# One kernel, one edit: where weight differences are taken and which queue carries a table

## The chip, the core and the metric

The kernel runs on one core of a Trainium2 chip. Its time is the device time of one execution in microseconds (us). A core has a matrix engine (TensorE, PE in the profile, with its weight loads as PEld), VectorE (DVE), ScalarE (ACT), GpSimd (POOL) and SyncE (SP). The engines run side by side, each takes its own instructions strictly in order, and they wait for each other through semaphores. SP computes nothing here; it issues transfers (DMAs). ACT can issue transfers too, from the same instruction stream that holds its activations and copies.

## What is computed

Only the first block of the reference matters for this change: three approximate matrix products ("amm"), each with a softmax over 16 codewords, with batch normalisation between them. The edit touches the first two of the three.

```python
def _amm(patches, centroids, lut, inv_temp):
    v = patches.reshape(B, ncb, sub, H * W).transpose(0, 3, 1, 2)
    scores = 2.0 * einsum('blcs,cks->blck', v, centroids) - sum(centroids * centroids, -1)
    attn = softmax(scores * inv_temp, axis=-1)
    out = einsum('blck,cko->blo', attn, lut)
...
out = _amm(x, c1_centroids, c1_lut, c1_invt)                    # layer 1
out = relu(_bn(out, bn1_g, bn1_b))
out = _amm(_extract3x3(out, 1), c2_centroids, c2_lut, c2_invt)  # layer 2
out = relu(_bn(out, bn2_g, bn2_b))
out = _amm(out, c3_centroids, c3_lut, c3_invt)
```

Since the 16 weights of a softmax add up to one, the kernel replaces the first 15 rows of every table block by their difference to row 15. Row 15 then drops out of the product, and its place is used for rows of another block.

## The kernel before

**Units.** Layer 1 and layer 2 are each cut into 128 units: 16 pairs of images times 8 tables. For unit u, PE makes scores (L910 in layer 1, L1056 in layer 2, four PSUM banks of the pool `sc`), ACT takes exponentials into a tile t (L576, four activations), DVE transposes and sums (L588, L607), takes reciprocals and spreads them (L609, L619), POOL multiplies (L621, L626), and PE multiplies the tile by table u % 8 (L748, 16 passes for four blocks or 12 for three). Six tiles t are in use; scores run four units ahead of the products.

**Rows.** Row 15 of each block of t is filled from a spare tile by SP: `spare_rows`, L725 (one transfer) or L728 (three transfers, for units 0, 4, 8, ...). A product can't begin before the rows of its own unit have landed.

**Tables.** `packed_lut` gives five steps for table b. `own` loads the 512 KB table (L692 in layer 2, four transfers of 128 KB). `less` takes the differences: two PE products of 128x512 with `less_last` (L700), each copied back over the table by ACT (L701). `keep` (only for b = 0 and 4) writes one block of the differenced table to DRAM (L704), and `others` reads rows of it into row 15 of the blocks of the other tables (L707). The products of table b need `less` of b and `others` of b. The PSUM of `less` comes from the pool `po` (3 banks) for b < 4, and from the 4 banks of `sc` for b > 3, the same banks that the scores use.

**Order in layer 1.** Steps are hung on the loop index i of `units` with `at(i, ...)`; the list at L858 gives the index at which table b is differenced. Within one i the order is: scores of unit i + 4, softmax and rows of earlier units, the steps hung on i, then a product. The products follow the rule `{-2: 0, -1: -1, 0: 1, 1: 2, 2: -1}`: unit 0 at i = -2, none at -1, unit 1 at 0, unit 2 at 1, none at 2, unit 3 at 3.

**Order in layer 2.** The input is first written to DRAM with borders (`store_pair`: an ACT activation at L990 into `pad`, then three SP transfers at L1002) and then read back as shifted patches (`load_patches`, L1012: six transfers per unit, four patch buffers). The first two units' patches are issued from SP and ACT together (`both`), all others from SP. `store_pair(0, 1)`, which units 4 to 7 need, is in `second_half` at i = -3; `more_tables` at i = -2 holds `others` of tables 2 and 3 and `own` of table 7. `side2` takes the differences of tables 4 to 7 at i = -3, -2, -1 and 0. `score2(u)` first issues the patches of unit u + 3 for u > 1, ahead of the rows that the same i issues.

**Completion semaphores.** The program gives transfers of SP and ACT eight completion semaphores in turn. So a transfer waits, besides its data, for the transfer that had its semaphore before, which in this stretch is the one eight issues earlier, on whichever of the two queues that was.

`exact` is a second pass of the same code that runs only if an overflow is found; it is not taken in the executions shown.

Of the kernel before, what the change touches and what calls it, by code (L numbers as in the profile page):

```python
# [149 lines left out]
def conv_preact_kernel(ctx: ExitStack, tc: tile.TileContext, a: dict, out: bass.AP):  # L150
    nc = tc.nc
    x = a["x"]
    B = x.shape[0]
    NP = B // 2
# [266 lines left out]
    lut2_tiles = a["lut2"].rearrange("(b c j e k) w -> b c (e k) j w", b=8, c=4, j=4, k=KC)  # L421
# [85 lines left out]
    def layers(exact, early=None):  # L507
# [151 lines left out]
        kept = two.enter_context(tc.tile_pool(name="p12x", bufs=1, side="right"))  # L659
# [19 lines left out]
        def packed_lut(layer, b):  # L679


            v = weights[b].rearrange("p (s w) -> p s w", s=4)
            kept = tables[2 * layer - 2 + b // 4].rearrange("(c k) w -> c k w", k=KC)
            j0 = 0 if b % 4 else 1
            k0 = b % 4 - 1 if b % 4 else 3

            def own():
                if layer == 1:
                    nc.sync.dma_start(v, lut1_tiles[b].rearrange("j c k w -> (c k) j w"))
                    return  # L690
                for c in range(4):
                    nc.sync.dma_start(v[32 * c : 32 * c + 32], lut2_tiles[b, c])  # L692

            def less():
                for h in range(2):
                    t = weights[b][:, 512 * h : 512 * h + 512]
                    ps = scores(512) if b > 3 else None
                    if ps is None:
                        ps = ps_po.tile([P, 512], F32, tag="po", name="less")
                    nc.tensor.matmul(ps, less_last, t, start=True, stop=True)  # L700
                    nc.scalar.copy(t, ps)  # L701

            def keep():
                nc.sync.dma_start(tables[2 * layer - 2 + b // 4], v[:, 0])  # L704

            def others():
                nc.sync.dma_start(v[15::16, j0:], kept[:, k0 : k0 + 13 - 4 * j0 : 4])  # L707

            return v, own, less, keep, others


# [82 lines left out]
        with ExitStack() as s:  # L794
# [56 lines left out]
            luts2 = [packed_lut(2, b) for b in range(8)]  # L851
# [3 lines left out]
                    at(8 * p + c - AHEAD - 1 - (p == 0), normalise(p, c))  # L855
            at(24, edges)
            at(40, masks2)
            for b, i in enumerate((-4, -4, -3, -3, -1, 0, 0, 1)):  # L858
                for k in (2, 3, 4):
                    if k != 3 or b % 4 == 0:  # L860
                        at(i, lambda b=b, k=k: luts[b][k]())
# [110 lines left out]
        with ExitStack() as s:  # L972
            st = s.enter_context(tc.tile_pool(name="p2tt", bufs=1 if exact else 2))
            once = s.enter_context(tc.tile_pool(name="p2c", bufs=1))
            luts3 = []

            NPB = 4
            SPAN = 2 * IMG - LEAD
            pbuf = []
            for k in range(NPB):  # L980
                t = once.tile([P, 4, 2 * IMG], F32, tag=f"patch{k}", name=f"patch{k}")
                nc.gpsimd.memset(t, 0.0)
                pbuf.append(t)
                if k == 0:
                    bn_final(once, stats1, 1, [1], sc1, bi1)
                    add_up(0, 8 * NP)

            def store_pair(p, h, engines=(nc.sync,)):
                t = pads[h]
                nc.scalar.activation(  # L990
                    t.rearrange("p (i r c) -> p i r c", r=15, c=15)[:, :, :14, :14],
                    out1[:, h, p * N2 : (p + 1) * N2].rearrange(
                        "p (i r c) -> p i r c", r=14, c=14
                    ),
                    AF.Relu,
                    bias=bi1[:, h : h + 1],
                    scale=sc1[:, h : h + 1],
                )
                for x in range(3):
                    c0 = LEAD + 2 * p * IMG + 1 - x  # L1000
                    v = h1d[x // 2][h, :, :, c0 : c0 + 2 * IMG]
                    engines[x % len(engines)].dma_start(v[:, x::2] if x < 2 else v, t)  # L1002

            def load_patches(u, engines=(nc.sync,)):
                p, b = divmod(u, 8)
                h, g = divmod(b, 4)
                for n, (src, rows) in enumerate(zip(h1d, (8, 16))):
                    for dy in range(3):  # L1010
                        c0 = LEAD + 2 * p * IMG + 15 * (dy - 1)
                        engines[dy % len(engines)].dma_start(  # L1012
                            pbuf[u % NPB][tap_row(dy, 2 * n) :: rows, :, :SPAN],
                            src[h, 4 * g : 4 * g + 4, :, c0 : c0 + SPAN].rearrange(
                                "q r n -> r q n"
                            ),
                        )

            both = nc.sync, nc.scalar
            store_pair(0, 0)  # L1020
            luts2[0][2]()
            luts2[1][2]()
            load_patches(0, engines=both)
            load_patches(1, engines=both)
            luts2[0][3]()
            luts2[2][2]()
            luts2[3][2]()
            load_patches(2)
            luts2[0][4]()
            load_patches(3)  # L1030

            def second_half():
                store_pair(0, 1)
                luts2[1][4]()
                if not exact:
                    load_patches(NPB)

            def more_tables():
                luts2[2][4]()
                luts2[3][4]()  # L1040
                luts2[7][1]()

            if exact:
                second_half()
                more_tables()
            w9, bias2 = parts[2]

            def score2(u):
                if u > (0 if exact else 1) and u + NPB - 1 < 8 * NP:
                    load_patches(u + NPB - 1)  # L1050
                scs = [scores(N2) for j in range(4)]
                for c in range(4):
                    for j, sc in enumerate(scs):
                        r = slice(32 * j, 32 * j + 27)
                        v = pbuf[u % NPB][r, c].rearrange("p (i r c) -> p i r c", r=15, c=15)
                        nc.tensor.matmul(  # L1056
                            sc[32 * c : 32 * c + 32],
                            w9[r, u % 8 * 4 + c],
                            v[:, :, :14, :14],
                            start=True,  # L1060
                            stop=True,
                        )
                return scs

            ahead = 1 if exact else 4

            def side2(i):

                if i == 1 - ahead and not exact:
                    second_half()  # L1070
                if i == 2 - ahead and not exact:
                    more_tables()
                for b in range(4, 8):
                    if i == max(b - 7, -ahead):
                        luts2[b][2]()
                    if i == max(b - 4, 0):
                        luts2[b][4]()
                if i == max(-2, -ahead):
                    luts2[4][3]()
                p = {4: 1}.get(i + ahead, (i + ahead + 9) / 8)  # L1080
                if p in range(1, NP):
                    for h in range(2):
                        store_pair(int(p), h)
                if i == 60:
                    bias3, biases = score_biases(ps_tr, big, st, 3, raw[3], P, 2, mask8, 4)
                    parts[3] = score_matrices(big, 3, "", raw[3], mask8), bias3
                    parts["biases3"] = biases
                if i == 64:
                    parts["biases3"]()
                next_lut3(i - 8 * (NP - 1) - 1)  # L1090

            def next_lut3(b):
                if b >= 0:
                    luts3.append(load_lut(b, a["lut3"][b * P : (b + 1) * P]))


            out2 = out1
            stats2 = big.tile([P, 2, NP, 6], F32, tag="stats", name="stats2")
            units(
                ahead,  # L1100
                ts,
                st,
                [v for v, *_ in luts2],
                score2,
                bias2,
                out2,
                stats2,
                side2,
                lambda h: bn_final(once, stats2, 2, [h], sc2, bi2),
                halve=not exact,  # L1110
            )
            next_lut3(7)
            add_up(1, 8 * NP)
# [402 lines left out]
    with ExitStack() as s:  # L1516
# [20 lines left out]
        for k in range(2):  # L1537
            t = once.tile([P, CT, LY], F32, tag=f"y{k}", name=f"y{k}")
            v = t[:, :, LEAD : LEAD + 2 * IMG]
# [562 lines left out]
        def store(p, h, xt, rank):  # L2102
# [33 lines left out]
            k0=41,  # L2136
# [167 lines left out]
```

## Time and profile before

| | us |
|---|---|
| median of 3 runs | 3368.95 |
| lowest and highest run | 3367.61, 3372.37 |
| the profiled execution, its own time | 3369.36 |
| its span, first to last instruction | 3367.6 |
| PE busy in it | 3297.9 (98%) |
| PE waits for a table of L692 (L700) | 6.7, one wait |
| PE waits for rows (L748 for t<-spare) | 5.5, four waits |
| mean granted TensorE clock | 0.994 |

A busy engine in this profile is one that has an instruction in flight. PE is busy nearly all the time, so in the two layers concerned the end can only move by what PE idles, or by the stretches in which its granted clock is halved. Both are found at the start of layer 1 (20 to 66 us from the start of the span) and at the start of layer 2 (826 to 910 us).

### The profile page before, as it was taken

Reading aid. Unit: us, or ns where it says so; the run is one execution under the profiler, and the core shown is the slowest. Engines: PE = TensorE matmul, PEld = TensorE weight load, DVE = VectorE, ACT = ScalarE, POOL = GpSimd, SP = SyncE. Lnnn points to the kernel's source line nnn. Section 1 sums busy time; section 2 is a strip of 40 time slices with the busy share of each in tenths; the row PEclk is TensorE's granted clock in tenths of the full one; section 3 lists DMA queues with packets and bytes.
Section 4 is the critical chain, followed back from the end, with each engine's and each line's share of the span. In section 5 each row is a group of like instructions: output and inputs, shape, how many; then the busy total and the mean of one; then the engine's idle time right before and its main releaser. Section 6 shows DMA issues by size and latency. Waiting matters only on the chain. (4 is left out here: it accounts for less than half of the span.)

```text
span 3367.6 us, 61031 instructions
## 1 busy us (share of the span) xinstructions
PE 3297.9 (98%) x22287; PEld 2011.5 (60%) x22287; DVE 2868.9 (85%) x4174; ACT 1788.6 (53%) x4419; POOL 2528.4 (75%) x1562
## 2 busy tenths in 40 slices
PE   7999999999899999999999999998999999999999
PEld 4555555554345444444478888885666666666665
DVE  8999999997788898888666667655899999999996
ACT  4555555554444444444311111107888888888886
POOL 5999999997688888888532222215988888888888
PEclk9999999999999999999999999999999999999999
DMA  4110111102444344343231111113233333232321
GB/s 120 47 49 28 46 47 34 40 28 78 136 126 122 112 120 123 109 125 109 69 81 50 50 50 39 50 47 125 67 88 98 90 89 98 78 91 84 93 81 49
DMA packets 242253, 266.34 MB, mean 79 GB/s; under 512 B 32812, under 2 KB 239700, under 8 KB 241944
## 3 DMA queue, kind: packets, MB, share of 16 engines
q1 hardware_dynamic: 241128, 261.85, 26.4%
q8 instruction: 180, 2.95, 0.4%
q14 instruction: 129, 1.06, 0.1%
q10 hardware_dynamic: 816, 0.48, 0.1%
HBM read 171.01 MB, written 75.58 MB: 73 GB/s over the span
## 5 line engine op out<-in xcount | busy, mean ns | idle before, releaser
L626 POOL TENSOR_TENSOR t<-t,r 128x1568 f32<-128x1568 f32 (+5 forms) x292 | 962.1, 3296 | 527.7 <-issue 222.7
L748 PE MATMUL po<-t,lut 128*128 128x392 f32 x3840 | 1332.2, 500 | 6.9 <-DMA t<-spare 5.5
L748 PEld LDWEIGHTS po<-t,lut 128*128 128x128 f32 x3840 | 710.6, 190 | 605.5 <-issue 81.3
L1811 PE MATMUL mm<-y,lut 128*128 128x392 f32 x2048 | 714.6, 494 | 2.0 <-DVE k L1827 2.0
L588 DVE STREAM_TRANSPOSE tt<-t 128x1568 f32<-128x1568 f32 (+1 forms) x284 | 517.4, 1822 | 158.5 <-ACT t L576 155.2
L576 ACT ACTIVATE t<-sc,cbias 128x392 f32<-128x392 f32 (+1 forms) x624 | 322.4, 597 | 557.0 <-PE sc L910 190.8
L2035 DVE SCALAR_TENSOR_TENSOR pa<-y,lepe_w,pa 128x406 f32<-128x406 f32 x900 | 536.4, 637 | 19.3 <-PE pa L2017 17.0
L619 DVE STREAM_TRANSPOSE r<-rc 128x1568 f32<-128x1568 f32 (+1 forms) x284 | 520.8, 1834 | 11.6 <-POOL t L626 1.2
L1811 PEld LDWEIGHTS mm<-y,lut 128*128 128x128 f32 x2048 | 369.4, 188 | 243.7 <-issue 6.3
L591 POOL TENSOR_TENSOR tt<-tt 128x784 f32<-128x784 f32 x252 | 463.5, 1839 | 24.0 <-DVE tt L588 21.5
L576 ACT ACTIVATE t<-sc,room 128x392 f32<-128x392 f32 x512 | 259.0, 588 | 391.9 <-issue 164.7
L1393 PE MATMUL po<-t,lut 128*128 128x224 f32 (+2 forms) x1352 | 313.3, 414 | 0.0
L607 DVE TENSOR_REDUCE sm<-tt 128x98 f32<-128x784 f32 (+2 forms) x284 | 297.0, 1046 | 1.3 <-POOL tt L591 0.8
L1393 PEld LDWEIGHTS po<-t,lut 128*128 128x128 f32 (+1 forms) x1352 | 233.4, 189 | 62.9 <-issue 60.6
L609 DVE RECIPROCAL rc<-sm 128x98 f32<-128x98 f32 (+1 forms) x284 | 220.1, 775 | 9.8
L630 ACT ACTIVATE sm<-sm 128x98 f32<-128x98 f32 (+1 forms) x284 | 85.1, 300 | 159.0 <-DVE rc L609 159.0
L1997 POOL TENSOR_TENSOR qr<-qr,zb 128x784 f32<-128x784 f32 x64 | 118.2, 1856 | 49.0 <-DMA zb<-zd 48.7
L1664 ACT ACTIVATE w<-x,tb,gn_a 128x196 f32<-128x196 f32 x248 | 128.4, 518 | 35.4 <-POOL y L1546 28.3
L1823 ACT ACTIVATE e<-e 128x392 f32<-128x392 f32 x256 | 134.4, 525 | 1.0
L1777 ACT ACTIVATE y<-x,gb,ga 128x196 f32<-128x196 f32 x256 | 123.3, 541 | 12.6 <-POOL gb L1740 12.6
L1406 DVE TENSOR_TENSOR o<-po,o 128x224 f32<-128x224 f32 (+1 forms) x156 | 81.6, 543 | 56.7 <-PE po L1393 51.9
L825 ACT ACTIVATE x<-x,gn_b,gn_a 128x196 f32<-128x196 f32 x256 | 127.6, 557 | 4.3 <-POOL gn_b L296 3.8
(215 smaller groups left out, 4510.6 us busy)
## 6 DMA issues: line engine op xcount, KB each, us to landing
patch<-h1d SPq DMA_DIRECT2D x382, 108.5 KB
x<-in_x_dram SPq DMA_DIRECT2D x32, 784.0 KB
o3d<-o SPq DMA_DIRECT2D x56, 448.0 KB
x<-in_x_dram SPq DMA_DIRECT2D x64, 392.0 KB
out_dram<-x SPq DMA_DIRECT2D x64, 392.0 KB
o<-o3d SPq DMA_DIRECT2D x62, 392.0 KB
h1d<-pad SPq DMA_DIRECT2D x96, 225.0 KB
patch<-h1d SPq DMA_DIRECT2D x382, 54.2 KB
```

The source lines that it names most:

```text
L576: nc.scalar.activation(t[:, j, : sc.shape[1]], sc, AF.Identity if exact else AF.Exp, bias=bias[:, j : j + 1],)
L588: nc.vector.transpose(tt, tf)
L591: nc.gpsimd.tensor_tensor(tv[:, :, :8], tv[:, :, :8], tv[:, :, 8:], ALU.add)
L607: nc.vector.tensor_reduce(sm, tv, AX.X, ALU.add)
L609: nc.vector.reciprocal(rc, sm)
L619: nc.vector.transpose(r, bc(rc, 2, KC))
L626: nc.gpsimd.tensor_tensor(v[:, c], v[:, c], r[:, c], ALU.mult)
L748: nc.tensor.matmul(po[h], luts[b][:, j, h * P : (h + 1) * P], ts[u % len(ts)][:, j, :N2], start=(b == 0 and j == j0), stop=(b == 7 and j = ...
L1393: nc.tensor.matmul(dst, w, x, start=start, stop=stop)
L1811: nc.tensor.matmul(pv(), w[kt][:, m0 : m0 + P], ywin(p, first + kt), start=(kt == 0), stop=(kt == 3),)
L1823: nc.scalar.activation(e(), e(), AF.Exp, scale=-1.0)
L2035: nc.vector.scalar_tensor_tensor(acc, neighbours(p, c, offset(k)), lw[:, c, k : k + 1], acc, ALU.mult, ALU.add,)
```

## The change

In layer 1 the differences of tables 5, 6 and 7, with their `others`, move from i = 0, 0 and 1 to i = 1, 2 and 3.

In layer 2:

- `own` of table 7 (four transfers) moves from SP at i = -2 to ACT's queue, directly after ACT's four patch transfers and ahead of the copies of tables 2 and 3.
- `others` of tables 0 to 3 (four transfers) move from SP to ACT's queue, all in `second_half`, ahead of the activation of `store_pair(0, 1)`. Before, that of table 0 stood on SP between the patches of units 2 and 3, that of table 1 after `store_pair(0, 1)`, and those of 2 and 3 in `more_tables`.
- The differences of tables 5, 6 and 7 move from i = -2, -1 and 0 to i = -1, 1 and 2. `others` stay at i = b - 4.
- The patches of unit 5 are no longer issued by `score2(2)`, ahead of the rows of unit 1, but after these rows, at the end of i = -2.

```diff
-            def own():
+            def own(engine=nc.sync):
                 if layer == 1:
                     nc.sync.dma_start(v, lut1_tiles[b].rearrange("j c k w -> (c k) j w"))
                     return
                 for c in range(4):
-                    nc.sync.dma_start(v[32 * c : 32 * c + 32], lut2_tiles[b, c])
+                    engine.dma_start(v[32 * c : 32 * c + 32], lut2_tiles[b, c])
...
-            def others():
-                nc.sync.dma_start(v[15::16, j0:], kept[:, k0 : k0 + 13 - 4 * j0 : 4])
+            def others(engine=nc.sync):
+                engine.dma_start(v[15::16, j0:], kept[:, k0 : k0 + 13 - 4 * j0 : 4])
...
-            for b, i in enumerate((-4, -4, -3, -3, -1, 0, 0, 1)):
+            for b, i in enumerate((-4, -4, -3, -3, -1, 1, 2, 3)):
                 for k in (2, 3, 4):
                     if k != 3 or b % 4 == 0:
                         at(i, lambda b=b, k=k: luts[b][k]())
...
             load_patches(0, engines=both)
             load_patches(1, engines=both)
+            luts2[7][1](nc.scalar)
             luts2[0][3]()
             luts2[2][2]()
             luts2[3][2]()
             load_patches(2)
-            luts2[0][4]()
             load_patches(3)
 
             def second_half():
+                for b in range(4):
+                    luts2[b][4](nc.scalar)
                 store_pair(0, 1)
-                luts2[1][4]()
                 if not exact:
                     load_patches(NPB)
 
-            def more_tables():
-                luts2[2][4]()
-                luts2[3][4]()
-                luts2[7][1]()
-
             if exact:
                 second_half()
-                more_tables()
...
             def score2(u):
-                if u > (0 if exact else 1) and u + NPB - 1 < 8 * NP:
+                if u > (0 if exact else 2) and u + NPB - 1 < 8 * NP:
                     load_patches(u + NPB - 1)
...
                 if i == 1 - ahead and not exact:
                     second_half()
                 if i == 2 - ahead and not exact:
-                    more_tables()
+                    load_patches(NPB + 1)
                 for b in range(4, 8):
-                    if i == max(b - 7, -ahead):
+                    if i == (max(b - 7, -ahead) if exact else (-3, -1, 1, 2)[b - 4]):
                         luts2[b][2]()
                     if i == max(b - 4, 0):
                         luts2[b][4]()
```

`luts2[b][1]` is `own`, `[2]` is `less`, `[3]` is `keep`, `[4]` is `others`.

## The prediction, made before the changed kernel was run

> **What bounds the kernel now.** First the page's busy line: PE is the bound, so I look only for PE idle time near the edited code.
>
> ```profile
> PE 3297.9 (98%) x22287; PEld 2011.5 (60%) x22287; DVE 2868.9 (85%) x4174; ACT 1788.6 (53%) x4419; POOL 2528.4 (75%) x1562
> ```
>
> Then the table of windows over the start of layer 2 (stretch, length, busy time and count of each engine, granted clock, DMA share, GB/s): PE is not full, and its clock drops twice.
>
> ```profile
> 830.00:840.00 10.00, 6.44 (x46) 1.84 (x45) 0.00 (x0) 4.76 (x9) 3.85 (x3) 0.78 0.56 161
> 840.00:850.00 10.00, 8.53 (x70) 2.49 (x66) 9.81 (x7) 6.08 (x13) 3.48 (x4) 0.70 0.30 83
> 850.00:860.00 10.00, 7.45 (x53) 3.16 (x53) 6.48 (x5) 4.42 (x10) 6.26 (x4) 1.00 0.46 138
> 860.00:870.00 10.00, 3.28 (x35) 1.39 (x36) 8.12 (x7) 2.56 (x7) 8.09 (x4) 0.65 0.55 155
> ```
>
> Then PE's timeline there: the waits are for a copy of ACT (834.92), for table 7 (867.65), and for rows of unit 6 (907.90). Products of units 0, 1, 2, 3 start at 850.38, 871.19, 878.44, 887.98.
>
> ```profile
> 834.92 1.37 PE L700 MATMUL less<-lut,less_last 128*128 128x512 f32 x2 [2.27 <-ACT lut L701]
> ...
> 850.38 4.19 PE L748 MATMUL po<-t,lut 128*128 128x392 f32 x12
> ...
> 867.65 3.75 PE L700 MATMUL sc<-lut,less_last 128*128 128x512 f32 x4 [6.72 <-DMA lut<-in_lut_dram]
> 871.19 6.44 PE L748 MATMUL po<-t,lut 128*128 128x392 f32 x16
> ...
> 887.98 5.53 PE L748 MATMUL po<-t,lut 128*128 128x392 f32 x16
> ...
> 907.90 5.50 PE L748 MATMUL po<-t,lut 128*128 128x392 f32 x16 [2.16 <-DMA t<-spare]
> ```
>
> Then the two issuing queues. SP is issuing almost without a gap from 848.56 to 874.75: 0.63 us per patch transfer, 0.6 per row or `others` transfer, 0.47 per quarter of a table.
>
> ```profile
> 848.56 2.52 SPq L728 DMA_DIRECT2D t<-spare  x3
> ...
> 863.53 1.87 SPq L692 DMA_DIRECT2D lut<-in_lut_dram  x4
> ...
> 865.97 8.68 SPq L1012 DMA_DIRECT2D patch<-h1d  x12
> 874.75 0.61 SPq L725 DMA_DIRECT2D t<-spare  x1
> ```
>
> ```profile
> 830.76 3.42 ACTq L1012 DMA_DIRECT2D patch<-h1d  x4
> 834.28 1.56 ACT L701 COPY lut<-less 128x512 f32<-128x512 f32 x3 [3.58 <-DMA patch<-h1d]
> ```
>
> ACT's copies stood still while ACT issued its four patch transfers, and PE at 834.92 waited for the first of them.
>
> **Layer 1.** The steps keep their number, so only PE's gaps count. Before, from PE's timeline: 0.66 at 39.31, 0.66 at 54.38, 0.72 at 63.66, and two scores stretched over PSUM banks (2.28 at 41.22 and 2.36 at 63.66 against 0.94, so 1.34 and 1.42): 4.8 us. After: three differences each stand behind a score and wait for its second exponential (3 x 0.66), as table 4's does (0.66); the stretch of 1.34 stays; unit 7's score now waits for table 6's copies (0.58 each), some 0.6: 4.6 us. The product of unit 1 comes out at 43.9 instead of 47.33, and its rows (issued 41.47, L725 landing 2.15 later: 43.6) are there. Value -0.2, bounds -1.4 (unit 7's stretch goes) and +1.0 (a full wait for the copies more).
>
> **Layer 2, step 1: `own` of table 7 on ACT.** ACT is done with its patches at 834.18. The listing of the changed program shows the four new transfers waiting for the semaphores of earlier ones: ACT's first, second and third patch transfer, and one of SP's. By the trace's landing records these came at 834.01, 835.29, 836.68 and 835.49. So the third issue starts at about 836.8; two at 0.45 (L692) end at 837.7. ACT issuing 128 KB of a table is not in the trace; bounds: 4 x 0.43 with no wait at all (835.9), and ACT's own patch rows (up to 1.29) for the last two (839.4). I take 837.7, the L692 row being the same transfer. Queued behind it: the copies of tables 2 and 3, then all exponentials. The copy at 834.28 comes at 837.8, +3.5, and PE's last difference, scores of units 0 and 1, their exponentials and unit 0's softmax move with it. The same listing ties SP's patch transfers of unit 1 to ACT's last one (landing 837.15); they land near 840.5, before the score needs them (839.12 + 3.5).
>
> **Step 2: `others` of tables 0 to 3 on ACT.** They stand behind unit 0's total (844.49 before, 848.0 after, 0.38 long). 848.4 + 4 x 0.6 (L707) = 850.8; the last lands 2.1 us after its issue: 852.3. Queued behind: `pad` (0.7), table 4's copies, and unit 2's score, which needs their banks (847.7 before, now near 853.5). That is no loss by itself, for the product of unit 0 needs rows: SP's later patches of unit 3 and the first rows of unit 0 wait, by the listing, for the semaphores of these very transfers, the first row for the last. It is issued at 852.8 instead of 848.56 (+4.2), and the product of unit 0 starts at 854.6 instead of 850.38, with table 5's difference (1.98) still ahead of it.
>
> **Step 3: what SP no longer issues.** From unit 0's first row to unit 2's row SP took 874.75 - 848.56 = 26.2 us. Out go `own` (863.53 to 865.50) and three `others` (1.8): 3.8; the new order of unit 5's patches and unit 1's rows changes no sum. 852.8 + 22.4 = 875.2, landing 2.2 later: the product of unit 2 starts at 877.4 against 878.44. PE gets there in time: unit 0's product to 858.8, score, 0.75, table 5 (1.98), score, unit 1's product at 864.6 (its rows: 852.8 + 1.9 + 1.35 + 1.4 waiting for the pad to land + 3.8 of patches + 2.2 = 863.5), score, 0.75, table 6: about 874, some 3 us of slack, which also cover a first half-rate stretch that lasts longer.
>
> **Step 4: what is late next.** Behind unit 2's product (5.5) now stand score 0.94, 0.75 + 1.98 for table 7, 1.07 for its copies and a score 0.95: unit 3's product at 888.6 against 887.98, +0.6. The wait of 6.72 for table 7 has become waits for ACT and SP. On to unit 6, before took 887.98 to 907.90 = 19.9 with the 2.16 in it. After: 888.6 + 17.8 = 906.4; unit 6's row, by SP's own rows from 875.2 (four groups of patches, two pairs of pads, five rows, three `others`: 28.5), is issued at 903.7 and lands at 905.9: no wait. So -1.5 in all, bounds: -4.4 if ACT isn't held in step 1 (first row at 850), +3 if each ACT issue costs as its slowest.
>
> TensorE's clock: windows 830 to 850 show 0.78 and 0.70 behind an idle time of only 2.27 us in one piece; behind 6 us I expect it at least as low, paid out of the slack of step 3. The Trainium skill (TensorE: Matmul & The Clock Gate, "Why this matters for your kernels") asks for no idle gaps over about 3 us between bursts; it speaks against step 1, and by it alone two new gaps each cost a stretch at half rate, about +3 us. The trace halves the clock on less idle than that, so the measurement rules here.
>
> The skill (DMA: Bandwidth & Descriptors, "Issuing engines are not separate DMA queues") says that a second issuing engine saves only sequencer time. In this stretch sequencer time is the scarce thing on SP (rows above), so the rule doesn't forbid the gain of step 3; it leaves the sum as it is.
>
> **Sum.** The profiled execution: span 3367.6 - 1.5 - 0.2 = 3365.9, with its 1.8 around it 3367.7. It stood 0.4 above the median of the runs, so the median becomes 3367.3. Behind 910 us PE is full, so the shift should last to the end.
>
> **Rivals.**
>
> *A, the edit does all it could* (0.12). Neither queue is held up; the waits at 867.65 (6.72), its slow passes (3.75 for 1.98, 6.44 for 5.53: 2.7), and 2.16 vanish: -11.6, 3357. For it: they are the largest idle rows. Against it: SP's 22.4 us from the first row on, which even with rows as early as before (848.56) put unit 2 at 873.1, -5.3 at most; and ACT's row at 834.28 shows issuing holds up copies.
>
> *B, the clock stays at half rate* (0.20). Every few us PE waits 0.75 to 3 us, no stretch is full, and from 846 to 877 the passes go at 0.65 (spacing of the slow loads at 871) instead of 0.345. Work there: 18.4 us, so +16, less the idle that it fills (3 before unit 0, 0.75 twice, 3.4 before unit 2): +8, 3376 after the gain above. It decides as soon as the clock is still half at 862. For it: 0.65 in 860 to 870 before. Against: the two drops before ended within about 10 us each, beside waits of the same kind.
>
> *C, the two queues block each other longer* (in the range). Every us that ACT is held at 834 or 848 goes through the semaphores to SP's rows one for one; from 5 us more on the sum is +3.5.
>
> **Numbers.** 0.2% is 6.7 us, about what a measurement of this kernel can tell from no change. My forecast, 3367.3, with 3363 to 3371 of its own, has 0.68 and lies within it: same 0.68, faster 0.12 (A), slower 0.20 (B, and C at its far end). The range 3361 to 3377 takes in B's price and half of A's.
>
> **What would show it.** Right: the wait of PE for a table at L700 gone; ACT's queue with eight new issues, the copy of table 2 near 837.8; SP's first row near 852.8 behind a pause in the patches of unit 3; unit 3's product within 2 us of 888.6; no wait of 2 us near 906. Wrong: unit 3's product at 883 or earlier (A), a clock of 0.5 to 0.6 in the windows 850 to 870 (B), or a PE gap anywhere behind 920 that the trace before doesn't have.

## The result and the profile after

The changed kernel took 3386.23 us (median of 6 runs, 3385.48 to 3388.08) against 3368.34 us (6 runs, 3367.11 to 3372.37) for the kernel before in the same series: a ratio of 1.0052, 95% interval 1.0039 to 1.0065. That is 17.9 us slower. The forecast was 3367.3 us, and its range ended at 3377. The profiled execution took 3385.66 us with a span of 3383.0 us, 15.4 us longer than the span before.

The page's busy line of the changed kernel shows 2.2 us more PE work in a span longer by 15.4 us; so PE idles more:

```profile
PE 3300.1 (98%) x22287; PEld 2012.1 (59%) x22287; DVE 2872.0 (85%) x4174; ACT 1789.7 (53%) x4419; POOL 2528.3 (75%) x1562
```

At the place that the edit touches, no loss of that size is found: between 830 and 870 us PE idles 12.45 us, against 14.30 in the same windows before. The table of windows of the changed kernel over the start of layer 2 (columns as before: stretch, length, busy time and count of PE, PEld, DVE, ACT, POOL, then granted clock, DMA share, GB/s):

```profile
830.00:840.00 10.00, 3.71 (x7) 0.96 (x5) 0.00 (x0) 1.56 (x3) 2.96 (x2) 0.76 0.57 163
840.00:850.00 10.00, 8.40 (x73) 2.22 (x72) 6.02 (x4) 5.01 (x11) 0.00 (x0) 0.73 0.29 77
850.00:860.00 10.00, 6.22 (x36) 2.81 (x37) 8.03 (x6) 3.96 (x9) 7.49 (x6) 0.66 0.35 113
860.00:870.00 10.00, 9.22 (x84) 3.81 (x83) 5.19 (x5) 6.07 (x14) 3.57 (x2) 1.00 0.50 138
```

PE's timeline of the changed kernel there, with the instructions that the prediction named:

```profile
838.07 2.07 PE L700 MATMUL less<-lut,less_last 128*128 128x512 f32 x2 [6.29 <-ACT lut L701]
...
855.87 5.80 PE L748 MATMUL po<-t,lut 128*128 128x392 f32 x12 [1.06 <-DMA t<-spare]
...
877.71 5.50 PE L748 MATMUL po<-t,lut 128*128 128x392 f32 x16 [1.69 <-DMA t<-spare]
...
888.45 5.53 PE L748 MATMUL po<-t,lut 128*128 128x392 f32 x16
...
906.15 5.54 PE L748 MATMUL po<-t,lut 128*128 128x392 f32 x16
```

The first row of unit 0 and the row of unit 2 on SP's queue of the changed kernel, whose issue times the prediction named:

```profile
853.76 1.98 SPq L728 DMA_DIRECT2D t<-spare  x3
...
875.39 0.61 SPq L725 DMA_DIRECT2D t<-spare  x1
```

and on ACT's queue the four `others`:

```profile
848.75 2.69 ACTq L707 DMA_DIRECT2D lut<-tables  x4
```

The wait of 6.72 us for table 7 is gone. A wait of 6.29 us for ACT's copies has come in earlier, and the clock is back at full rate by 860. The product at 906.15 has no wait, where the one before, at 907.90, had 2.16 us.

To see where the two executions part, I took the same PE instruction in both traces (same tile, same count), and the difference of their starts, after minus before:

| at (us) | 120 | 780 | 920 | 2270 | 2320 | last PE instruction | end of the span |
|---|---|---|---|---|---|---|---|
| after minus before (us) | -0.9 | -0.9 | -1.7 | -2.9 | -1.9 | +10.9 | +15.4 |

For the first 2320 us the changed kernel is ahead. All of the loss, 1.9 + 15.4 = 17.3 us, comes behind that, in the last block of the program, the attention, which no line of the edit touches. In the traces PE's idle time between 2310 and 3300 us is 8.7 us before and 17.6 us after, spread over the whole stretch, and from PE's last instruction to the end of the span it is 7.7 us before and 12.2 us after. The list of waits in the attention block (engine, what it waited for, total us, times, longest) of the kernel before:

```profile
POOL qr L1997 <- DMA zb<-zd: 48.7, 20, 5.7
...
POOL x L2072 <- ACT side L2064: 20.3, 4, 7.0
```

and of the changed kernel, whose line numbers there are 5 lower:

```profile
POOL x L2067 <- ACT side L2059: 45.0, 15, 10.2
POOL qr L1992 <- DMA zb<-zd: 25.7, 14, 7.7
```

A wait that occurs 4 times in one program and 15 times in the other suggests that the instructions stand in another order. Compared one by one, they do: DVE's 2062 instructions of this block stand in a different order in the two traces, from some 45 us into the block (2332 us in the changed kernel's trace) on.

The order is made by a planner in the kernel's own Python code, `Plan`, which hands out the pieces of the attention block to the engines as they come free in a simulated run. Its `write` holds these lines:

```python
engines = {p[0] for p in self.pieces}
...
for e in engines:
    if free[e] > now:
        continue
    ...
        if locked and any(t > now for o, t in port.items() if o != e):
            rest.append((r, n))
            continue
        piece = n
```

`engines` is a set of strings. The order in which Python walks through such a set is drawn anew for each process that generates the program. The planner lets certain pieces of DVE and POOL (`locked` in the code) run only one at a time, as if through one port: of two such pieces that are ready at the same planned moment, the engine asked first gets it. Running the planner with all 120 orders of the five names gives only two different programs: 60 orders with DVE asked before POOL, and 60 with POOL before DVE. In the planner's own simulated time, which `write` returns, the block ends at 1084.8 us in the first and at 1102.7 us in the second, with and without the edit: 17.9 us apart before any chip is involved. The trace of the kernel before has the first program's order in all 2062 DVE instructions of the block, the trace of the changed kernel the second's. So the suspicion was that the measured difference was not one of the edit at all.

### The profile page after: what moved, and what is told of

It is laid out like the page before. It is cut to its first block, busy times and chain, and to the rows that moved or that the text cites. A ratio compares the mean times of both kernels' runs of the same rounds, so it can differ in the third digit from the quotient of the medians.

```text
span 3383.0 us, 61034 instructions
## 1 busy us (share of the span) xinstructions
PE 3300.1 (98%) x22287; PEld 2012.1 (59%) x22287; DVE 2872.0 (85%) x4174; ACT 1789.7 (53%) x4419; POOL 2528.3 (75%) x1562
## 5 line engine op out<-in xcount | busy, mean ns | idle before, releaser
L619 DVE STREAM_TRANSPOSE r<-rc 128x1568 f32<-128x1568 f32 (+1 forms) x284 | 520.8, 1834 | 11.6 <-POOL t L626 1.2
```

Source lines behind the costliest of these rows:

```text
L619: nc.vector.transpose(r, bc(rc, 2, KC))
```

## The experiments

All of them write the set's order out, so that the edit and the order can be told apart. "Same position" below means how far PE's shift against the trace compared with changes between 780 and 920 us, which is the start of layer 2 without what happened ahead of it.

**Edit and order, taken apart.** Four kernels, each with one line of `Plan.write` changed:

```diff
-        engines = {p[0] for p in self.pieces}
+        engines = ("PE", "DVE", "ACT", "POOL", "SP")
```

or, for the other order, `("PE", "POOL", "ACT", "DVE", "SP")`.

The changed kernel, DVE first:

> The changed kernel with one line more: the planner of the attention block visits its engines in the written order PE, DVE, ACT, POOL, SP, where it took them from a set of strings, whose order changes from one build to the next. Theory (the 17 us are the planner's order, which the edit doesn't touch): from 2300 us on the instructions of the attention block stand in the order of the kernel before, and the time is 3365.5 to 3367.5 us, 0.9 to 2.9 us less than the kernel before. Rival (the edit itself costs them, by what it makes the attention block meet or by a clock that falls elsewhere): the time stays at 3386 us, whatever the order.

The kernel before, POOL first:

> The kernel before, untouched but for the planner's engines, written out as PE, POOL, ACT, DVE, SP. Theory: the attention block comes out in the order that the changed kernel's profile shows, and the time is 3385 to 3388 us, 17 to 20 us more than before, without any of the edit. Rival: it stays at 3368 us within 2 us.

The kernel before, DVE first:

> The kernel before with the planner's engines written out as PE, DVE, ACT, POOL, SP: a control. Both theories: 3368 us within 1 us, since this is the order that the profile of the kernel before shows. Anything else would mean that the written order isn't the one that was profiled.

The changed kernel, POOL first:

> The changed kernel with the planner's engines written out as PE, POOL, ACT, DVE, SP, which makes the square of edit and order complete. Theory (order alone): 3386 to 3389 us, as the kernel before with that order (3389.2 us) less the 0 to 3 us of the edit. Rival (edit and order act together): more than 3 us away from that.

In these series "the kernel before" was generated anew and run beside them. The same text that had taken 3368.34 us now took 3387.72, 3388.31 and 3387.43 us in three series on three chips. Its ratio is the yardstick across the chips:

| | median us (runs) | ratio to the kernel before as generated for that series | 95% interval |
|---|---|---|---|
| before, DVE first | 3370.89 (5) | 0.9950 | 0.9937 to 0.9964 |
| changed, DVE first | 3370.73 (5) | 0.9948 | 0.9934 to 0.9961 |
| before, POOL first | 3389.16 (11) | 1.0003 | 0.9994 to 1.0012 |
| changed, POOL first | 3390.28 (11) | 1.0003 | 0.9994 to 1.0012 |

The order is worth 18 us without the edit (3389.16 - 3370.89, one chip) and some 19 with it (0.0055 in the ratios; the two medians are from two chips). The edit is worth nothing that can be measured in either order. The first theory holds and the rival is out. The order of DVE's instructions in the block is that of the first profile in both traces with DVE first, and that of the changed kernel's first profile in both with POOL first, and the waits follow it. The kernel before with POOL first:

```profile
POOL x L2072 <- ACT side L2064: 45.0, 16, 10.2
```

The changed kernel with DVE first:

```profile
POOL x L2067 <- ACT side L2059: 20.0, 3, 7.0
```

All four expected times were too low by 1 to 3 us: the changed kernel with DVE first was to take 3365.5 to 3367.5 us and took 3370.73 (3366.55 to 3372.78); the control, expected at 3368 within 1, took 3370.89 (3370.35 to 3373.36); the two with POOL first were to take at most 3388 and 3389. The order of DVE's instructions in the control and its waits (POOL for `x` 20.0 us, 3 times) are those of the first profile. Why these series ran slower than the first was not tried apart.

**Layer 1 alone** (DVE first; before, with the list at L858 of the change):

```diff
-            for b, i in enumerate((-4, -4, -3, -3, -1, 0, 0, 1)):
+            for b, i in enumerate((-4, -4, -3, -3, -1, 1, 2, 3)):
```

> The control with layer 1's part of the change alone (differences of tables 5, 6 and 7 behind scores 1, 2 and 3). By the prediction's sum for layer 1: -0.2 us, bounds -1.4 to +1.0, so 3367 to 3369 us, not to be told from the control. Rival (a late difference makes PE wait for its table in layer 1, some 2 us each): 3370 us or more, with a wait of PE for a layer-1 table in the profile.

3368.49 us (3366.29 to 3372.18) against the control's 3370.89 (3370.35 to 3373.36): the ranges overlap, and no PE wait for a table of layer 1 appeared. An effect of a few tenths can't be seen here. Eleven of the profiled executions have the same layer 1, and in them PE at 120 us stands anywhere from 1.2 us earlier to 3.7 us later than in the changed kernel with DVE first.

**Step 1, the early transfer of table 7 on ACT's queue.** From here on all kernels are the changed one with DVE first, and are compared with its 3370.73 us.

```diff
-            luts2[7][1](nc.scalar)
             luts2[0][3]()
             luts2[2][2]()
             luts2[3][2]()
+            luts2[7][1](nc.scalar)
```

> The changed kernel with the planner's written order (DVE before POOL) and table 7's own transfer put on ScalarE's queue behind the copies of tables 2 and 3 instead of ahead of them. Step 1 of the prediction (the four issues hold ScalarE for 3.5 us, all the rest of the start of layer 2 comes later by as much): the first copy of table 2 comes at about 834 us instead of 837.5, PE's last difference no longer waits 6.3 us for ScalarE, TensorE has unit 0's product 2 to 3.5 us earlier, and the time is 1 to 3 us below that of the changed kernel with the same order, 3370.7 us. Rival (the start waits for the transfers of the rows and of the tables, not for ScalarE): the copies come earlier, but PE at 950 us stands within 0.5 us of where it stood, and the time is the same within 1 us.

3362.88 us (3360.65 to 3369.64), ratio 0.9930 (0.9917 to 0.9944): 7.9 us below, more than expected. In the same position PE stands 4.5 us earlier. ACT's timeline of this kernel:

```profile
830.03 3.42 ACTq L1012 DMA_DIRECT2D patch<-h1d  x4
833.54 1.56 ACT L701 COPY lut<-less 128x512 f32<-128x512 f32 x3 [3.56 <-DMA patch<-h1d]
835.34 0.59 ACT L701 COPY lut<-less 128x512 f32<-128x512 f32 x1 [0.24 <-PE less L700]
835.35 1.91 ACTq L692 DMA_DIRECT2D lut<-in_lut_dram  x4
```

In the changed kernel's first trace the same queue reads:

```profile
829.88 3.42 ACTq L1012 DMA_DIRECT2D patch<-h1d  x4
833.34 4.00 ACTq L692 DMA_DIRECT2D lut<-in_lut_dram  x4
837.43 1.56 ACT L701 COPY lut<-less 128x512 f32<-128x512 f32 x3 [7.61 <-DMA lut<-in_lut_dram]
```

The four issues themselves take 1.91 us when they come later; of the 4.00 us ahead of the copies (3.63 in the trace with DVE first) about half is waiting for the semaphores of the patch transfers. With them behind, the copies come as early as before the change, PE's wait for ACT falls from 5.9 us (changed, DVE first) to 2.3 us, and unit 0's product starts at 852.70 instead of 856.51 (1.1 us of that from ahead of layer 2), though PE now waits 3.88 us for unit 1's patch, which it did not before. The rival is out. Of the 7.9 us, 4.5 lie here by this pair of traces; the rest is the spread of the start, described below, and what one profile can't resolve.

One limit holds for all shifts against the changed kernel with DVE first. Three traces have its code of layer 2, and in the same position the first profile stands 1.2 us and the one with POOL first 1.4 us earlier than this one, whose unit 2 met a lower clock:

```profile
878.50 7.20 PE L748 MATMUL po<-t,lut 128*128 128x392 f32 x16 [2.05 <-DMA t<-spare]
```

The other two took 5.50 us for it. So a shift of 1.4 us is not resolved. The 4.5 us are 3.2 to 3.3 against the other two traces, and the hold of ACT still costs more than the limit.

Two more places for that transfer. On ACT's queue behind the four `others`:

```diff
-            luts2[7][1](nc.scalar)
...
                 for b in range(4):
                     luts2[b][4](nc.scalar)
+                luts2[7][1](nc.scalar)
```

> The changed kernel with the planner's written order and table 7's own transfer on ScalarE's queue behind the four transfers of the kept rows, some 16 us later than in the changed kernel and some 13 us later than behind the copies of tables 2 and 3, where the kernel took 3362.9 us and TensorE stood 4.5 us earlier at 920 us, counted from the same point ahead of layer 2. Theory (the early transfer costs by holding ScalarE and by sharing the queue with the first patches): the wait for unit 1's patch, 3.9 us there, goes too, and the time is 1 to 3 us below 3362.9 us. Rival (the end of the start is set by unit 0's rows, which come through the spare buffer in DRAM): PE waits there instead, time within 1 us of 3362.9. Second rival: the issues hold the padded copy and unit 2's activations, 1 to 3 us above.

3366.16 us (3363.16 to 3367.50); same position: 2.6 us earlier (1.2 and 1.3 against the other two traces). Unit 1's wait of 3.88 us for its patch is gone, as the theory says, but the issues now stand ahead of `pad` and table 4's copies, and unit 2's score waits for these, in PE's timeline of this kernel:

```profile
851.61 2.09 PE L1051 MATMUL sc<-patch,room 27*32 27x392 f32 x28 [4.41 <-ACT lut L701]
```

The second rival named the mechanism; the median is 3.3 us above 3362.88, just past its 1 to 3. And on SyncE's queue, behind `load_patches(3)`, nothing of it on ACT:

> The changed kernel with the planner's written order and table 7's own transfer on SyncE's queue, behind the patches of units 2 and 3, and nothing of it on ScalarE's. Theory (ScalarE held is the whole loss of step 1): the copies of table 2 start at about 834 us, and the time is within 1.5 us of 3362.9. Rival (four issues on SyncE push the rows and patches behind them back by 2 to 4 us): PE waits longer for unit 0's rows, and the time is 2 to 4 us above 3362.9.

3363.75 us (3363.41 to 3365.29), within 0.9 us of the place behind the copies; same position: 5.0 us earlier (3.6 and 3.8 against the other two traces). The theory holds in its result: what the early transfer cost goes when ACT is no longer held. In both places the table's data also flow later, past the first patches, and this was not tried apart. The wait for unit 0's rows does grow, to 3.58 us from 0.93, but unit 0's product still starts earlier than with the early transfer, at 855.38 against 856.51.

**Step 2, `others` of tables 0 to 3 on ACT's queue.** Back to SyncE:

```diff
-                    luts2[b][4](nc.scalar)
+                    luts2[b][4]()
```

With table 7's transfer early on ACT, as in the change:

> The changed kernel with the planner's written order, and the four transfers of the kept rows into tables 0 to 3 on SyncE's queue again, at their place in the order, instead of on ScalarE's. Step 2 of the prediction (four issues of some 0.7 us, 2.7 us in all, ahead of the padded copy on ScalarE): ScalarE's padded copy starts some 2.7 us earlier than at 851.5 us, while the first row's transfers on SyncE stay behind the tables' issues; time 0 to 2 us below 3370.7 us. Rival (what ScalarE gains SyncE loses: the issues hold up the patches and rows there): same time within 1 us, with unit 0's rows later by 1 to 3 us.

3373.64 us (3368.28 to 3374.41); same position: 1.7 us later. With table 7's transfer behind the copies:

> Table 7's own transfer behind the copies of tables 2 and 3 on ScalarE's queue, and the kept rows' transfers into tables 0 to 3 on SyncE's queue; written order. With the own transfer early, the move to SyncE gave PE a wait of 6.0 us for a table and TensorE stood 1.7 us later at 920 us, counted from the same point ahead of layer 2. Theory (the kept rows are on the path at either place): the same wait, shorter, and 0.5 to 2.5 us above 3362.9. Rival: the earlier copies give enough room, and the time is within 0.5 us of 3362.9 or below.

3366.81 us (3360.52 to 3369.29), 3.9 us above 3362.88; same position: 2.7 us later than there. In both, unit 0's product no longer waits for rows but for its table, in PE's timeline of the first

```profile
857.59 6.78 PE L748 MATMUL po<-t,lut 128*128 128x392 f32 x12 [5.95 <-DMA lut<-tables]
```

and by 3.52 us in the second. In the first, neither the gain expected by step 2 nor the rival's 1 us came, but a loss of 2.9 us in the median and 1.7 in the trace (2.9 and 3.0 against the other two traces). For the second, the theory named the wait and the sign and was 1.4 us short in the median; 1.7 of the 2.7 us in its trace are one product at the lower clock (7.20 us for 5.50). The new wait is shown in both. That the move of `others` to ACT's queue pays, some 1 to 3 us in the traces, is likely and not shown by the runs: the ratios (0.9954 against 0.9948, 0.9935 against 0.9930) lie well within each other's intervals.

**Step 4, the later differences of layer 2.** Back to the units of the kernel before:

```diff
-                    if i == (max(b - 7, -ahead) if exact else (-3, -1, 1, 2)[b - 4]):
+                    if i == max(b - 7, -ahead):
```

With table 7's transfer early on ACT:

> The changed kernel with the planner's written order, and layer 2's differences of tables 4 to 7 behind the scores that they stood behind before (units -3, -2, -1 and 0 in place of -3, -1, 1 and 2). Step 4 of the prediction (the later place takes 1.7 us out of units 3 to 6): PE waits again for a table that comes late, 2 to 7 us at the difference of table 6 or 7, and the time is 1 to 2 us above 3370.7 us. Rival (table 7's own transfer, early on ScalarE's queue, already takes that wait away): no such wait, the same time within 1 us.

3370.93 us (3366.18 to 3373.20); same position: 1.0 us earlier (0.3 and 0.4 later against the other two traces, so nothing resolved). No wait for a table: the rival was right, and the early transfer alone takes that wait away. With the transfer behind the copies:

> Table 7's own transfer behind the copies of tables 2 and 3 on ScalarE's queue, and layer 2's differences of tables 4 to 7 at the units of the kernel before (-3, -2, -1, 0); written order. Theory (once table 7 is fetched on ScalarE's queue, the differences' places are worth nothing): 3362.9 us within 1.5 us, and no wait of PE for a table. Rival (the later places pay): a wait of PE for table 6 or 7 of 1 us or more, and 1 to 3 us above 3362.9.

3367.30 us (3363.00 to 3371.66), 4.4 us above 3362.88; same position: 3.7 us later than there. The theory (within 1.5 us) was wrong, and the price is above the rival's 1 to 3 us, but its wait for a table isn't there. PE waits for the rows of unit 6 instead, and the product behind that wait runs 7.20 us in place of 5.53:

```profile
909.88 7.20 PE L748 MATMUL po<-t,lut 128*128 128x392 f32 x16 [1.98 <-DMA t<-spare]
```

So in these traces the later differences pay only once table 7 no longer holds ACT. How much is not shown: 1.7 of the 3.7 us are that product's lower clock, and the ratios, 0.9934 (0.9920 to 0.9948) against 0.9930, don't separate the two versions. What the new order of unit 5's patches is worth was not tried apart. The best versions found keep all of the edit except that one place: 3362.88 and 3363.75 us, ratios 0.9930 (0.9917 to 0.9944 and 0.9916 to 0.9943) where both kernels in their better order have 0.9950 and 0.9948. That is some 6 us below both, and 23 below the changed kernel as first measured. The intervals overlap; the shifts in the traces, 3.2 to 5.0 us against the three of the changed code and 4.1 and 4.6 us against the kernel before with DVE first, are the firmer part of it.

## Why the prediction was wrong

**The step that failed** is the last sentence of the sum: "Behind 910 us PE is full, so the shift should last to the end." PE there is nearly full in one given program. The sentence took for granted that the program behind the edited lines is the same in both kernels, and it was not: the planner of the attention block had drawn its other order, 17.9 us by the medians of the result, 18 us by the two kernels without the edit. No rival held this. One of the signs named for a wrong prediction did: "a PE gap anywhere behind 920 that the trace before doesn't have". With the order fixed, the edit moves the median by -0.2 us (DVE first) and the ratio by 0.0000 (POOL first). The forecast of -1.65 us can't be told from that: each ratio is known to some 0.09 to 0.14%, which is 3 to 5 us.

Point by point, from the changed kernel's first trace; to compare with the predicted times, remember that it runs 0.9 us ahead from 120 us on.

- *Layer 1, -0.2*: -0.9 at 120 us, of which 0.5 was already there at PE's first product, ahead of the edit. Unit 1's product came at 43.88, where 43.9 was forecast. Three differences waited behind their scores (0.66, 0.66 and 0.72 us), where the sum had four. Its value is neither shown nor refuted.
- *Step 1, the copy of table 2 at 837.8*: 837.43. Right in mechanism, some 0.5 us short in size: four issues of 4.00 us.
- *Step 2, first row issued at 852.8, product of unit 0 at 854.6*: 853.76 and 855.87, so 1.9 and 2.2 us later than the sum once the 0.9 is counted. On top of step 1's 0.5, unit 0's total came 10.9 us behind the copy (837.43 to 848.35) where the sum took 10.2, the four issues of `others` took 2.69 us instead of 2.4, and the first row was issued 2.3 us behind the last of them instead of 2.0.
- *Step 3, unit 2's row at 875.2, product at 877.4*: 875.39 and 877.71, 1.1 us later than the sum with the 0.9 counted: SP made up part of what step 2 had missed, since the 22.4 us taken for its path were 21.6.
- *Step 4, unit 3's product at 888.6, unit 6's at 906.4 without a wait*: 888.45 and 906.15, no wait, 0.7 us later than the sum with the 0.9 counted. From 780 to 920 us the shift is -0.9 us in this pair of traces, +0.4 and -0.7 in the two pairs with a fixed order: a mean of -0.4, where -1.5 was forecast. So the terms of steps 1 and 2 were too small by 1.9 us together, and step 3 gave back a part.
- *The bound of -4.4 "if ACT isn't held in step 1"*: with the hold taken away PE stood 4.1 us (behind the copies) and 4.6 us (on SyncE) earlier than in the kernel before with DVE first, in the same position. The prediction had priced the flaw of the edit, but did not draw the conclusion that it was one.
- *Rival A* (all waits vanish, -11.6): the wait at 867 went, but one of 6.29 us for ACT came. *Rival B* (half rate for longer): the windows show 0.76, 0.73, 0.66 and then 1.00 where 860 to 870 had 0.65 before. By the clock records of the traces the half rate between 830 and 880 us lasted 17.1 us after and 20.5 before. *Rival C* needed a hold of 5 us more; steps 1 and 2 together missed by 2.
- *The Trainium skill's rule on the clock* (TensorE: Matmul & The Clock Gate, "Why this matters for your kernels"), by which the prediction estimated that two new gaps would each cost a stretch at half rate, some +3 us: the rule names gaps of over about 3 us, and of the new gaps, 6.29 and 2.76 us, only the first is one, while one of 6.72 us went. The first pair of traces shows no added half rate, as the last point says. The other two pairs don't settle it: between 800 and 910 us they have 23.9 us of half rate after against 17.1 before (DVE first), and 23.9 against 23.9 (POOL first).

The cause of the 17.9 us is shown, by writing the order out in both kernels. That the second order is the longer one the planner's own simulation says too, by 17.9 us; that the figures agree so closely may be chance. Which pieces in it cost the time is only read from the waits (POOL for `x` 45 us instead of 20, a longer tail), and was not tried apart.

## What to carry to other kernels

Before a difference is explained by an edit, compare the order of all instructions in the two programs outside the edited lines, and generate the same text twice: a planner or scheduler that walks through a set, or breaks ties by anything not written down, can be worth more than the edit. Here it was 18 us against an edit of about zero.

A transfer issued from ACT held ACT here for the issue and for the semaphores that the transfer waited for. Put such a transfer behind the copies that the critical engine waits for: four issues took 3.63 and 4.00 us ahead of them and 1.91 us behind. An edit that sums to nothing may be parts that pay and one that costs, which only undoing the parts one at a time shows.

## What the runs showed of the hardware beyond that

The clock falls at different places in executions whose program is the same up to there. In the first 120 us, the version with table 7 behind the copies was granted the full clock in every window of 10 us. The version with the early differences, which has the same layer 1, had 0.84, 0.82, 0.88 and 0.95 in the windows from 10, 20, 40 and 50 us. PE stood 4.8 us later there at 120 us. In the clock records the half rate came in stretches of 3.41 us or multiples of it, but for the last, which the end of the program cuts off. A pause of about 2 us was sometimes followed by one and sometimes not: behind pauses of 1.98, 2.05 and 2.80 us the next product of 16 passes took 7.20 us, behind 2.09, 2.16 and 2.35 us it took 5.50. That spread is why single effects here are read from the shift between two points of a trace as well as from medians of five runs. The shift still holds the clock's luck between its two points, 1.7 us for one such product.
